# The planner's time allowance for the loads of x that the layer-norm statistics read

## The chip, the cores and the metric

The kernel runs on one core of one Trainium2 chip. The metric is device time in microseconds (us) of one execution, as the median of several runs. A profile is one further execution with its own time.

The engines are named as the profile names them: PE (TensorE, with PEld for its weight loads and PEclk for the clock it was granted), DVE (VectorE), ACT (ScalarE), POOL (GpSimd) and SP (SyncE, which here only issues transfers; "SPq" is its queue).

## The reference

Four layers of graph attention run one after another on 128 graphs of 64 nodes with 512 features, all in float32. Each layer adds to `x` what an attention makes of `h = relu(layernorm(x))`. The graph's adjacency masks the scores. Cut to what matters:

```
h = max(layernorm(x), 0);  x = x + gnn0(h)   # q,k,v (8 heads of 64), masked softmax, values
h = max(layernorm(x), 0);  x = x + gnn1(h)   # the same, and an output projection Wo + bo
h = max(layernorm(x), 0);  x = x + gnn2(h)   # q k^T times adj^T, each row over its norm, times v
h = max(layernorm(x), 0);  x = x + gnn3(h)   # softmax attention, projection o, then o + layernorm(o)
return x
```

`layernorm(x)` is `(x - mean) / sqrt(var + 1e-5)` over the 512 features of a node. The first step of every layer is therefore a read of `x` for mean and variance.

## The kernel before

**Tiling.** The 8192 rows (128 graphs times 64 nodes) are cut into 16 blocks of 512 rows, and a block into four tiles of 128 rows. The four layers make 64 blocks, numbered `n` from 0 to 63; `n // 16` is the layer. `x` between the layers stands in HBM: the input, then a buffer `x1_k` for each block, then the output. Block `n + 1` is loaded and normalized while block `n` is projected.

**One block's way to TensorE.** `load_x` issues four transfers on SP, one for each 128x512 tile `xin` (a ring of four buffers, so a tile of the next block can be loaded only when the tile before it in the same buffer has been used). `layer_norm` takes `bn_stats` and `bn_aggr` of each tile on DVE, then `ve` and `rs = ve ** -0.5` on POOL for the four tiles together, then `nb = -mean * rs` on DVE. ACT then overwrites each tile by `relu(rs * xin + nb)`. `turn` transposes it: DVE splits it into 16-bit halves `z`, SP issues a transposing transfer `hp<-z`, and ACT puts the halves together in `hT`. `sums_x` makes four sums and differences of quarters of `hT` on POOL, the tile `S`.

**Projections.** Each 512x512 weight product is done with seven block products instead of eight, and some of those again with seven quarter products. So PE reads `hT`, `S` and prepared sums of weights, and DVE, ACT and POOL put the partial results together from PSUM (tiles `u`, `s`, `z`, `q`, then `qT`, `kT`, `v`). There are eight PSUM buffers `mm`. Scores, softmax and values follow a block later, interleaved with the next block's projections.

**What sets the order.** Nothing is issued as the code meets it. `Plan.record` writes down every operation with what it depends on, a duration (`duration`, numbers set by hand) and a `late`: how long after the end of the instruction another engine can use the result. `Plan.order` then goes through all steps as a list scheduler: it keeps a time at which each of the five engines is free, picks the step that can start first, and among those that can start, the one of lowest `rank` (its place in the program, moved up for steps that read PSUM or are marked hot). `Plan.issue` issues the steps in that order, so each engine's instruction list is fixed at build time. On the chip every engine runs its own list in that order, and semaphores make it wait for the data. The planner's times are used for nothing else.

For a transfer on SP, `late` comes from line 213, which lets transfers follow each other at 280 bytes a ns (170 for transposes) and start 1400 ns after issue at the earliest, and from line 214, which adds an allowance: `MARGIN` (2000 ns, line 283) for a transposing transfer and 600 ns for every other one. A tile of 128x512 float32 is 262144 bytes.

```
            elif e == "sync":
                moved = max(moved, at + 1400) + late / (170 if calls[0][2].get("transpose") else 280)
                late = moved + (MARGIN if calls[0][2].get("transpose") else 600) - at - busy
```

In addition a transfer depends on the sixteenth-last product that the program recorded before it (`AHEAD`), so that loads aren't issued much too early.

All instructions are issued by `Plan.issue`, so the profile gives line 234 for nearly all of them; they are told apart by their tiles.

Of the kernel before, what the change touches and what calls it, by code (L numbers as in the profile page):

```python
# [59 lines left out]
class Plan:  # L60
# [96 lines left out]
    def order(self):  # L157
        n = len(self.steps)
        wait = [0] * n
        users = [[] for _ in range(n)]  # L160
        for i, s in enumerate(self.steps):
            lags = {**self.lags.get(i, {}), **{d: 0.0 for d in s[2]}}
            wait[i] = len(lags)
            for d, lag in lags.items():
                users[d].append((i, lag))


        rank = [
            i - (n if i in self.front else 0)
            - RUSH * (i in self.hot or any(  # L170
                v.tensor.name.startswith("mm_") for c in s[1] for v in c[1][1:] if isinstance(v, bass.AP)
            ))
            for i, s in enumerate(self.steps)
        ]
        ready = [0.0] * n
        free = {e: 0.0 for e in ("tensor", "vector", "scalar", "gpsimd", "sync")}
        added = 0.0
        moved = 0.0
        port = 0.0
        soon = {e: [] for e in free}  # L180
        here = {e: [] for e in free}
        for i in range(n):
            if not wait[i]:
                heapq.heappush(soon[self.steps[i][0]], (0.0, rank[i], i))
        out = []
        while len(out) < n:
            best = None
            for e in free:
                while soon[e] and soon[e][0][0] <= free[e]:
                    heapq.heappush(here[e], heapq.heappop(soon[e])[1:])  # L190
                if here[e]:
                    at = free[e]
                elif soon[e]:
                    at = soon[e][0][0]
                else:
                    continue
                if best is None or at < best[0]:
                    best = (at, e)
            at, e = best
            if not here[e]:  # L200
                while soon[e] and soon[e][0][0] <= at:
                    heapq.heappush(here[e], heapq.heappop(soon[e])[1:])
            i = heapq.heappop(here[e])[1]
            eng, calls, _, busy, late = self.steps[i]
            moves = calls[0][0] == "dma_start"
            if e == "gpsimd":
                busy += max(0.0, port - at)
            if moves and e == "gpsimd":
                moved = max(moved, at) + 8000
                added = max(added + 6000, at + 8500)  # L210
                late = added - at - busy
            elif e == "sync":
                moved = max(moved, at + 1400) + late / (170 if calls[0][2].get("transpose") else 280)
                late = moved + (MARGIN if calls[0][2].get("transpose") else 600) - at - busy
            elif e == "vector" and late == PORT:
                busy += max(0.0, free["gpsimd"] - at)
                port = at + busy
            free[e] = at + busy
            out.append((at, i))
            for u, lag in users[i]:  # L220
                same = self.steps[u][0] == e
                ready[u] = max(ready[u], at + busy - lag + (0.0 if same and not moves else late))
                wait[u] -= 1
                if not wait[u]:
                    heapq.heappush(soon[self.steps[u][0]], (ready[u], rank[u], u))
        self.start = {i: at for at, i in out}
        self.span = max(free.values())
        return [i for _, i in sorted(out)]
# [54 lines left out]
MARGIN = 2000  # L283
# [1090 lines left out]
```

## Time and profile before

| | |
|---|---|
| median of 3 runs | 2813.59 us (2810.73 to 2822.84) |
| the profiled execution's own time | 2814.77 us |
| its span, first to last instruction | 2813.0 us |
| granted PE clock over the span | 0.999 |
| loads of `xin` | 256, of 256 KB each, on SP |
| DMA, mean over the span | 122 GB/s |

The page's second part cuts the span into 40 equal slices of some 70 us. The layers end at about 690, 1500 and 1960 us. The lines are the busy tenths of each engine, the granted clock in tenths, and what the DMA engines moved:

```profile
PE   9999999999999999999999999999999999999998
DVE  8787576777668778777686665666678778777777
POOL 5666776779767768778689655455777877787875
PEclk9999999999999999999999999999999999999999
GB/s 161 134 155 150 118 178 117 131 147 166 76 111 87 116 93 124 91 97 115 98 133 149 169 168 138 158 143 172 114 80 87 118 93 91 121 104 80 131 78 95
```

A row of the waits reads "engine and tile that waited <- engine and tile (or transfer) that ended the wait: total us, how many times, longest us". A row of the timeline reads "start us, us, engine, line, operation, tile written<-tiles read, shape, count", and in brackets the idle time of the engine before it with what ended it.

### The profile page before, as it was taken

What the parts mean: (1) busy time and instruction counts of PE and PEld (TensorE: products, weight loads), DVE (VectorE), ACT (ScalarE), POOL (GpSimd) and SP (SyncE); (2) the same over time, 40 slices, a digit from 0 to 9 for tenths busy, and PEclk for the clock granted to TensorE, in tenths of its full rate; (3) what the DMA queues carried; (4) which work ended last, traced back from release to release, by engine and by line L of the source; (5) the groups of instructions that cost most, each with busy time, mean ns of one, the idle gap of its engine ahead of it and who ended that gap; (6) DMA issues with size and microseconds to landing.
All of it is one profiled execution on the core that took longest, in us unless ns stands there. A gap on an engine that the chain in (4) does not pass through costs nothing.

```text
span 2813.0 us, 67184 instructions
## 1 busy us (share of the span) xinstructions
PE 2795.0 (99%) x27264; PEld 2484.1 (88%) x27264; DVE 2059.2 (73%) x3900; ACT 1500.7 (53%) x2207; POOL 2014.5 (72%) x2061
## 2 busy tenths in 40 slices
PE   9999999999999999999999999999999999999998
PEld 8888888888889999999998888888888888888887
DVE  8787576777668778777686665666678778777777
ACT  5667566666464554554654444443545545555552
POOL 5666776779767768778689655455777877787875
PEclk9999999999999999999999999999999999999999
DMA  6566485567464656446567775666544644654644
GB/s 161 134 155 150 118 178 117 131 147 166 76 111 87 116 93 124 91 97 115 98 133 149 169 168 138 158 143 172 114 80 87 118 93 91 121 104 80 131 78 95
DMA packets 634599, 343.65 MB, mean 122 GB/s; under 512 B 484273, under 2 KB 565681, under 8 KB 634289
## 3 DMA queue, kind: packets, MB, share of 16 engines
q1 hardware_dynamic: 601024, 273.30, 43.1%
q0 software_dynamic: 33264, 66.06, 14.2%
q8 instruction: 213, 3.49, 0.5%
q14 instruction: 98, 0.79, 0.1%
HBM read 120.10 MB, written 102.76 MB: 79 GB/s over the span
## 4 chain that ended last, share of the span: by engine, by line
PE 95%; DVE 2%; POOL 1%; DMA 1%; issue 1%; SPq 0%; ACT 0%; POOLq 0%; DVEq 0%; ACTq 0%
PE mm L234 95%; SPq L234 0%; POOL S L234 0%; DMA w<-in_L_gnn_Wv_dram 0%; DMA w<-in_L_gnn_Wq_dram 0%; DMA xin<-x 0%; DVE xo L234 0%; DVE sr L234 0%; DVE z L234 0%; POOL rn L234 0%; DVE st L234 0%; DVE qT L234 0%; DVE q L234 0%; DVE w L234 0%; POOL w L234 0%
## 5 line engine op out<-in xcount | busy, mean ns | idle before, releaser
L234 PE MATMUL mm<-S,w 128*128 128x256 f32 (+1 forms) x3680 | 841.6, 377 | 2.0 <-DVE u L234 1.6
L234 PEld LDWEIGHTS mm<-S,w 128*128 128x128 f32 x3680 | 679.8, 190 | 88.6 <-issue 2.3
L234 PE MATMUL mm<-hT,w 128*128 128x256 f32 (+1 forms) x3256 | 601.5, 328 | 3.1 <-DVE q L234 2.8
L234 PEld LDWEIGHTS mm<-hT,w 128*128 128x128 f32 x3256 | 521.8, 191 | 58.6 <-DVE q L234 4.0
L234 DVE TENSOR_TENSOR u<-mm,s 128x512 f32<-128x512 f32 x414 | 284.4, 687 | 292.9 <-PE mm L234 245.3
L234 PE MATMUL mm<-w,S 128*128 128x256 f32 (+1 forms) x2096 | 488.4, 379 | 0.8 <-issue 0.8
L234 PEld LDWEIGHTS mm<-w,S 128*128 128x128 f32 x2096 | 384.2, 190 | 49.9 <-issue 1.2
L234 ACT COPY hT<-hp 128x1024 uint16<-128x1024 uint16 x252 | 330.2, 1358 | 45.3 <-DMA hp<-z 45.1
L234 PE MATMUL mm<-w,hT 128*128 128x256 f32 (+1 forms) x1804 | 346.7, 331 | 0.9 <-DVE q L234 0.8
L234 PEld LDWEIGHTS mm<-w,hT 128*128 128x128 f32 x1804 | 292.8, 191 | 33.7 <-DVE q L234 3.6
L234 DVE COPY z<-xin 128x1024 uint16<-128x1024 uint16 x252 | 255.0, 1023 | 35.4 <-ACT xin L234 29.4
L234 ACT COPY s<-mm 128x512 f32<-128x512 f32 x211 | 123.1, 585 | 288.7 <-PE mm L234 152.9
L234 ACT COPY s<-hp 128x1024 uint16<-128x1024 uint16 x188 | 244.4, 1349 | 3.9 <-DMA hp<-z 3.9
L234 ACT ACTIVATE xin<-xin,nb,rs 128x512 f32<-128x512 f32 x256 | 196.2, 813 | 86.6 <-DVE nb L234 86.6
L234 PE MATMUL mm<-w,SO 128*128 128x256 f32 x992 | 227.1, 379 | 0.0
L234 POOL TENSOR_TENSOR kT<-u,z 128x512 f32<-128x512 f32 x63 | 87.9, 1395 | 182.5 <-DVE u L234 112.7
L234 ACT COPY z<-s 128x1024 uint16<-128x1024 uint16 x188 | 189.6, 1047 | 41.7 <-POOL s L234 41.6
L234 PEld LDWEIGHTS mm<-w,SO 128*128 128x128 f32 x992 | 185.0, 190 | 23.3
L234 POOL TENSOR_TENSOR s<-s,sr 128x1024 f32<-128x1024 f32 x96 | 185.7, 1941 | 25.2 <-DVE nb L234 16.0
L234 POOL TENSOR_TENSOR S<-hT 128x512 f32<-128x512 f32 x126 | 170.3, 1351 | 42.9 <-ACT hT L234 42.9
L234 POOL TENSOR_TENSOR s<-s,mx 128x1024 f32<-128x1024 f32 x96 | 189.5, 2031 | 14.7 <-DVE mx L234 14.7
L234 DVE TENSOR_TENSOR q<-mm,q 128x128 f32<-128x128 f32 x402 | 113.9, 283 | 112.1 <-ACT q L234 96.9
(142 smaller groups left out, 4505.0 us busy)
## 6 DMA issues: line engine op xcount, KB each, us to landing
xin<-x SPq DMA_DIRECT2D x128, 256.0 KB, 3.5
xin<-in_x_dram SPq DMA_DIRECT2D x64, 256.0 KB, 3.4
x<-row POOLq DMA_DIRECT2D x16, 1024.0 KB, 13.4
xin<-out_dram SPq DMA_DIRECT2D x64, 256.0 KB, 4.2
out_dram<-row POOLq DMA_DIRECT2D x16, 1024.0 KB, 14.5
x<-xo POOLq DMA_DIRECT2D x15, 1024.0 KB, 9.3
out_dram<-xo POOLq DMA_DIRECT2D x15, 1024.0 KB, 10.2
xo<-in_x_dram SPq DMA_DIRECT2D x32, 256.0 KB, 4.2
```

What stands on the lines that cost most here:

```text
L234: getattr(getattr(self.nc, eng), op)(*a, **k)
```

## The change

The allowance of 2000 ns, until now for transposing transfers alone, is also used for the loads whose target is a tile `xin`, if the planner places them after its first 20 us. Other loads (weights, rows, `xo`) and the stores keep 600 ns. The condition stands in `Plan.order`:

```
-                late = moved + (MARGIN if calls[0][2].get("transpose") else 600) - at - busy
+
+                margin = calls[0][2].get("transpose") or calls[0][1][0].tensor.name.startswith("xin") and at > 2e4
+                late = moved + (MARGIN if margin else 600) - at - busy
```

The set of instructions, their dependences and their buffers are the same in both kernels. What can differ is the place of each instruction in its engine's list.

## The prediction

> **What bounds the kernel now.** I read the page first, then the waits of TensorE, then the waits of VectorE and the tile `xin`, and last the order of time around the one place where all of them meet. On the page:
>
> ```profile
> span 2813.0 us, 67184 instructions
> PE 2795.0 (99%) x27264; PEld 2484.1 (88%) x27264; DVE 2059.2 (73%) x3900; ACT 1500.7 (53%) x2207; POOL 2014.5 (72%) x2061
> ```
>
> TensorE is busy for 2795.0 of 2813.0 us, and VectorE, the engine that takes the statistics, for 73%. So a wait of VectorE costs time only where it holds up a PSUM eviction long enough to stop TensorE. What TensorE waited for in the whole run:
>
> ```profile
> PE mm L234 <- DVE q L234: 3.6, 3, 2.8
> PE mm L234 <- issue: 2.2, 2, 1.5
> PE mm L234 <- DVE u L234: 1.6, 2, 1.4
> PE mm L234 <- POOL ident masks.py:199: 1.4, 1, 1.4
> PE mm L234 <- DVE v L234: 0.7, 1, 0.7
> PE mm L234 <- ACT z L234: 0.4, 1, 0.4
> PE mm L234 <- ACT oT L234: 0.2, 1, 0.2
> PE mm L234 <- ACT hT L234: 0.2, 1, 0.2
> ```
>
> The columns are total us, times, longest. They sum to 10.3 us: this is all that any better order could take from TensorE by removing such waits, 0.37% of the span. Only the rows that name VectorE's evictions `q` and `u` (5.2 us) can come from a late load of `xin`. VectorE itself waited for those loads in 24 places:
>
> ```profile
> DVE st L234 <- DMA xin<-x: 22.2, 17, 5.4
> DVE st L234 <- DMA xin<-in_x_dram: 5.4, 4, 3.6
> DVE st L234 <- DMA xin<-out_dram: 2.9, 3, 1.2
> DMA to landing us min/median/max: 2.7/3.5/9.9
> ```
>
> Together 30.5 us, before 24 of 256 statistics; the last line is the loads' time from issue to landing. Lines 213 and 214 let the order expect a load 1400 + 262144/280 + 600 ns = 2.94 us after its issue, when nothing is queued ahead of it; half the loads land later than 3.5. The place where one of these waits reaches TensorE, in order of time (start, us, engine, what; in brackets the idle time before it and what ended it), and then the stretches around it, whose last three columns are granted clock, DMA share and GB/s:
>
> ```profile
> 1678.89 0.58 SPq L234 DMA_DIRECT2D xin<-x  x1
> ...
> 1684.26 0.69 DVE L234 BATCH_NORM_STATS2 st<-xin 128x6 f32<-128x512 f32 x1 [3.94 <-DMA xin<-x]
> 1684.87 0.27 DVE L234 TENSOR_TENSOR q<-mm,q 128x128 f32<-128x128 f32 x1
> ...
> 1685.19 0.57 PE L234 MATMUL mm<-hT,w 128*128 128x128 f32 x2 [2.83 <-DVE q L234]
> ```
>
> ```profile
> 1670.00:1690.00 20.00, 17.17 (x82) 14.89 (x81) 12.70 (x25) 8.29 (x12) 12.81 (x14) 0.91 0.93 211
> 1690.00:1735.00 45.00, 44.73 (x409) 39.00 (x408) 27.89 (x68) 16.75 (x26) 25.89 (x30) 1.00 0.53 134
> ```
>
> The load takes 5.34 us (issue at 1678.89 to the statistics at 1684.26), VectorE stands for 3.94 us with the eviction `q` behind it, TensorE stands for 2.83 us, and in these 20 us the granted clock is 0.91 against 1.00 in the next stretch. A pause here costs its length and then some slow matmuls.
>
> **The change, part by part.** It adds no instruction and takes none away. MARGIN is 2000 where 600 stood, so the order now expects a load of `xin` 1.40 us later, 4.34 us after its issue; only loads that the order places in its first 20 us keep the 600. Every step keeps its semaphores, so no wait is added. Everything else follows from the order made with that. I compared the two programs' orders engine by engine: TensorE's last difference is at row 3879 of 6174, VectorE's at 2631 of 3813, ScalarE's at 1377 of 1960, GpSimd's at 1127 of 1780, SyncE's at 683 of 1022. So layer 3, the last third of the time, is as it was and costs nothing either way.
>
> *Removed: VectorE's waits.* A wait of 3.94 us of which 1.40 us is now filled with other work leaves 2.5; TensorE's 2.83 us become 1.4. That is the lower bound of this gain at that place, 1.4 us. The upper bound is the whole of it, 2.83 us and the clock: (1 - 0.91) x 20 us = 1.8 us, together 4.6 us. At 463 us a like case, the statistics 1.39 us late by a load of 3.06 us, stopped TensorE for 0.5 us; 1.39 is under 1.40, so this one goes. Upper bound of all: 5.1 us. The other 22 waits of VectorE hide behind TensorE's queued matmuls, are worth nothing now and nothing when they are gone; the work that hides them is up to eight PSUM banks, and where that cover is gone the price is the one just read, 4.6 us. I take 3.5 us, nearer to the upper end because the neighbouring rows change too: on SyncE the transposes `hp<-z` around this load are put in another order.
>
> The Trainium skill, DMA: Bandwidth & Descriptors, section on the anatomy of one DMA, speaks against the change: a fit of about 2.0 us plus bytes over 436e3, for the software path; for 256 KB an estimate of 2.6 us, by which the old allowance would do and this gain would be zero. The measured medians here, 3.5 us and the 5.34 us of the load that matters, decide against that reading. The skill's TensorE: Matmul & The Clock Gate, part 1, says the clock falls after an idle window of some 3.4 us; the pause here was 2.83 us by the row and the clock fell to 0.91 all the same. By the rule the pause would be worth 2.8 us, by the row 4.6 us.
>
> *Moved: the statistics, and what hangs on them.* Of each block, four BATCH_NORM_STATS2 (0.68 us) and their aggregates move down VectorE's list; behind them stand `ve`, `rs` on GpSimd, `nb`, four activations, four `z` copies, four transposes on SyncE, four `hT` copies on ScalarE, and the sums `S` on GpSimd that TensorE reads. In layers 0 and 2 GpSimd's list changes most: where the four sums `S` (1.27 us each) stood ahead of the two row-max subtractions of the scores (1.90 us each), they now stand behind them in several early blocks. On SyncE the loads of the third and fourth `xin` tile, which stood ahead of the six loads of `xo` in layer 0, now stand behind them; an issue takes about 0.6 us, so 3.7 us. In the old order these sums had time:
>
> ```profile
> 118.70 1.27 POOL L234 TENSOR_TENSOR S<-hT 128x512 f32<-128x512 f32 x1
> 120.06 1.28 POOL L234 TENSOR_TENSOR S<-S,hT 128x512 f32<-128x512 f32 x1
> ...
> 133.42 3.62 PE L234 MATMUL mm<-S,w 128*128 128x256 f32 x16
> ```
>
> The second sum ends at 121.34 and is first read at 133.42, a lead of 12.1 us; sums 3.8 us (two subtractions) and statistics 1.4 to 5 us later still leave a few us. I take zero for layer 0 and keep 1.4 us for each of six blocks, 8.4 us, as the other end. At the entry of layer 2 the lead is thin already:
>
> ```profile
> 1588.57 1.27 POOL L234 TENSOR_TENSOR S<-hT 128x512 f32<-128x512 f32 x1 [4.21 <-ACT hT L234]
> ...
> 1590.59 1.67 PE L234 MATMUL mm<-S,w 128*128 128x256 f32 x7
> ```
>
> The sum ends at 1589.84 and is read 0.75 us later. A chain that is 1.40 us later costs 0.65 us here; five such blocks at the entry give 3.2 us, at worst five times 1.40, 7.0 us; at best nothing, if the list gains elsewhere what it loses there. I take 1.5 us. The end of the run is unchanged.
>
> **Sum.** The profiled execution took 2814.77 us (span 2813.0 and 1.8 around it). Less 3.5, plus 1.5: 2812.8 us. The median of the runs shown, 2813.59, is 1.2 us below that execution, so the forecast is 2811.6, rounded to 2812 us.
>
> **Rivals.** What a measurement of this kernel can tell from no change is about 0.5%, 14.1 us.
>
> *A, forecast: a small gain, 2812 us* (own range 2806 to 2818). For it: the wait at 1684 is in the chain that ended last, and the order now leaves room for it. Chance 0.40.
>
> *B, a wash: 2815 us.* The load at 1678.89 took 5.34 us, over 4.34, so the pause stays in part (1.4 us gained), and the entry of layer 2 pays 3.2 us; 2813.6 - 1.4 + 3.2 = 2815.4. For it: landings up to 9.9 us, and thin leads at 1590. Against: only a few loads exceed 4.34 by much. The change would then do what it says for VectorE and nothing for TensorE. Chance 0.30.
>
> *C, slower: thin leads turn into pauses with a slowed clock, 2832 us.* The place is the first blocks of layer 0, where the sums now stand behind the subtractions, and the entry of layer 2. As long as a sum is under a us late it costs that; a pause of near 3 us costs 4.6 us as at 1684. It decides from the fourth such pause on: 4 x 4.6 = 18.4 us over 2813.6. For it: one late load can delay all that hangs on it, and `xin`'s third and fourth tile are now issued later. Against: the lead of 12.1 us. Chance 0.22.
>
> *D, faster beyond the measurement: 2799 us.* It would need 14.1 us, where all waits of TensorE are 10.3 us and the clock lost at 1684 is 1.8 us; 12.1 us in all, 2801.5 us. So this needs short gaps inside the matmul stream to close too, which nothing in the profile ties to these loads. Chance 0.08.
>
> **How the numbers follow.** A and B lie within 0.5%: same 0.70; slower is C, 0.22; faster is D, 0.08. The range reaches from all of the gain, 2813.6 - 5.1 = 2808.5, less the 2.9 us by which the lowest run lies below the median, 2805.6, up to no gain with both worst costs, 2813.6 + 7.0 + 8.4 = 2829.0. C begins where it exceeds the measurement, at 2827.7, and its middle is 2832; to leave out no more than D and about half of C, under 2 in 10, I give 2805 to 2831.
>
> **What would show it.** Right: VectorE's waits for `xin` fall from 30.5 us to under 15; the row `PE mm <- DVE q` falls from 3.6 us to about 1; the clock in the stretch around 1680 us is nearer to 1.00; TensorE busy stays within a few us of 2795. Wrong in the step on sums: rows `PE mm <- POOL S` or `ACT hT` that are not there now, in layer 0 before 450 us or at 1500 to 1620 us, and stretches there with a clock under 1.00. Wrong in the first step: the pause at 1684 stands with the same load ahead of it. What makes the whole wrong is several new pauses of about 3 us.

## The result, and the profile after

| | before | after |
|---|---|---|
| median of 22 runs each, same chip | 2812.33 us (2810.69 to 2822.84) | 2817.61 us (2815.90 to 2819.64) |
| after / before, 95% interval | | 1.0016 [1.0009, 1.0023] |
| own time of the profiled execution | 2814.77 us | 2818.18 us |
| its span | 2813.0 us | 2816.4 us |
| granted PE clock over the span | 0.999 | 0.999 |

The changed kernel is slower by 0.16%. The interval excludes both a gain and a loss of 0.5%: small, but not of the sign that was forecast. In the first part of the page, the span and the busy times of the engines:

```profile
span 2816.4 us, 67187 instructions
PE 2794.6 (99%) x27264; PEld 2484.0 (88%) x27264; DVE 2033.6 (72%) x3900; ACT 1498.8 (53%) x2207; POOL 2012.9 (71%) x2061
```

TensorE is busy for 0.4 us less than before (2795.0) and the span is 3.4 us longer: the work did not grow, the gaps did. VectorE's waits for the loads of `xin`, after (total us, times, longest):

```profile
DVE st L236 <- DMA xin<-in_x_dram: 8.6, 4, 3.4
DVE st L236 <- DMA xin<-x: 4.4, 8, 1.2
DVE st L236 <- DMA xin<-out_dram: 2.6, 3, 1.1
```

They went from 30.5 us in 24 places to 15.6 us in 15, so the allowance did what it says. What TensorE waited for, after:

```profile
PE mm L236 <- DVE q L236: 7.3, 6, 4.4
PE mm L236 <- issue: 1.9, 2, 0.9
PE mm L236 <- POOL ident masks.py:199: 1.4, 1, 1.4
PE mm L236 <- ACT xin L236: 0.7, 2, 0.5
PE mm L236 <- DVE v L236: 0.7, 1, 0.7
PE mm L236 <- POOL SO L236: 0.7, 1, 0.7
PE mm L236 <- POOL hT L236: 0.6, 1, 0.6
```

The row for the evictions `q` was to fall from 3.6 us to about 1. It rose to 7.3, and one wait in it is of 4.4 us. It does not lie at 1684 us. The windows of after around the old place and around the new one (window; wall and PE busy; PEld; DVE; ACT; POOL; then granted clock, DMA share and GB/s):

```profile
860.00:880.00 20.00, 15.61 (x72) 13.55 (x71) 15.60 (x23) 4.89 (x8) 15.09 (x16) 0.91 0.63 105
...
1670.00:1690.00 20.00, 20.00 (x197) 17.75 (x196) 12.48 (x32) 7.86 (x15) 11.91 (x14) 1.00 0.53 145
```

The pause at 1684 is gone, and its stretch has the full clock. A larger pause stands in the middle of layer 1, where the same 20 us were full before:

```profile
860.00:880.00 20.00, 20.00 (x112) 18.09 (x111) 14.01 (x29) 10.66 (x19) 16.23 (x18) 1.00 0.78 132
```

**Where the 3.4 us come from.** TensorE has the same 27264 matmuls in every kernel, so the time that it loses can be worked out from the trace: the distance between the starts of two neighbouring groups of matmuls, less the first quartile of that distance over all groups of the same size, summed by stretch. It counts pauses as well as matmuls slowed by the clock. In every kernel of this study the span is 2770.7 us plus the total of this table (all in us):

| stretch | before | after | difference |
|---|---|---|---|
| 0–40 | 3.2 | 3.3 | +0.1 |
| 40–300 (layer 0) | 4.2 | 6.4 | +2.2 |
| 300–600 (layer 0) | 5.2 | 4.9 | −0.3 |
| 600–850 | 5.2 | 4.8 | −0.4 |
| **850–900 (layer 1)** | **0.4** | **6.5** | **+6.1** |
| 900–1500 | 4.8 | 5.0 | +0.2 |
| 1500–1650 (entry of layer 2) | 1.8 | 3.0 | +1.2 |
| **1650–1750 (layer 2)** | **6.2** | **0.6** | **−5.6** |
| 1750–1960 | 2.4 | 1.6 | −0.8 |
| 1960–2780 and end | 8.9 | 9.5 | +0.6 |
| total | 42.3 | 45.7 | +3.4 |

So the gain is there, and larger than the 3.5 us that the sum took; one single place in layer 1 takes all of it back, and layer 0 and the entry of layer 2 cost a little more.

**The place in layer 1.** VectorE and GpSimd in the order of time, before (start us, us, engine, line, operation, tile<-tiles read, shape):

```profile
862.34 1.34 POOL L234 DMA_DIRECT2D x<-xo  x1
...
862.50 0.28 DVE L234 TENSOR_TENSOR w<-w 128x128 f32<-128x128 f32 x1
...
863.99 4.79 POOL L234 TENSOR_TENSOR s<-s,mx 128x1024 f32<-128x1024 f32 x2
```

and after:

```profile
863.76 1.35 POOL L236 DMA_DIRECT2D x<-xo  x1
...
864.26 6.10 DVE L236 TENSOR_TENSOR w<-w 128x128 f32<-128x128 f32 x1
...
864.64 1.78 POOL L236 DMA_DIRECT2D x<-row  x1
...
865.41 4.79 POOL L236 TENSOR_TENSOR s<-s,mx 128x1024 f32<-128x1024 f32 x2
...
871.95 0.27 DVE L236 TENSOR_TENSOR q<-mm,q 128x128 f32<-128x128 f32 x1
...
872.28 1.65 PE L236 MATMUL mm<-w,oT 128*128 128x128 f32 x6 [4.39 <-DVE q L236]
```

The instruction `w<-w` is one of the sums of weights that are made once per layer, 128x128, both operands in SBUF, the on-chip buffer in which `xin` stands too. Before, it started 0.16 us after GpSimd's first transfer issue and took 0.28 us. After, it started 0.50 us after that issue and took 6.10 us: until GpSimd was through with two transfer issues and both row-max subtractions (865.41 + 4.79 = 870.20). The eviction `q` stands behind it and behind two statistics (871.95), and TensorE stands for 4.39 us. No load is late here, and no sum `S` either. The prediction had no term for this.

### The profile page after: what moved, and what is told of

Read it like the earlier page. It is cut to its first block, busy times and chain, and to the rows that moved or that the text cites. A ratio compares the mean times of both kernels' runs of the same rounds, so it can differ in the third digit from the quotient of the medians.

```text
span 2816.4 us, 67187 instructions
## 1 busy us (share of the span) xinstructions
PE 2794.6 (99%) x27264; PEld 2484.0 (88%) x27264; DVE 2033.6 (72%) x3900; ACT 1498.8 (53%) x2207; POOL 2012.9 (71%) x2061
## 5 line engine op out<-in xcount | busy, mean ns | idle before, releaser
L236 DVE COPY z<-xin 128x1024 uint16<-128x1024 uint16 x252 | 238.0, 958 | 41.7 <-ACT xin L236 31.5
L236 POOL TENSOR_TENSOR s<-s,sr 128x1024 f32<-128x1024 f32 x96 | 183.8, 1923 | 24.0 <-DVE nb L236 15.6
L236 PE MATMUL mm<-w,oT 128*128 128x256 f32 (+1 forms) x994 | 188.1, 335 | 4.6 <-DVE q L236 4.4
```

The lines of the kernel that those rows point to most:

```text
L236: getattr(getattr(self.nc, eng), op)(*a, **k)
```

## The experiments

All were timed in 11 runs beside 33 of the kernel before on the same chip (median 2813.80 us for the first four, 2813.65 for the last four). The theory: an engine's list decides what an eviction waits behind, and the cost is VectorE instructions that GpSimd holds up, standing ahead of an eviction `q`. The rivals: later statistics make the sums `S` late (the prediction's own third case), and the size of the allowance itself is the dose.

### e3_layer2: the allowance in layer 2 alone

```
-                margin = calls[0][2].get("transpose") or calls[0][1][0].tensor.name.startswith("xin") and at > 2e4
+                margin = calls[0][2].get("transpose") or calls[0][1][0].tensor.name.startswith("xin") and at > 1.48e6
```

> The larger allowance is used for the loads of layer 2 alone. The order of layers 0 and 1 is then that of the kernel before, the order of layer 2 that of the kernel after. Theory (three separate places: a gain at the entry of layer 2, one long wait of VectorE for GpSimd in layer 1, thin leads in layer 0): the pause of TensorE near 1684 us is gone and the one near 866 us does not come, so the time is 4.7 us below the kernel before, near 2807.6 us, and the row PE mm <- DVE q falls from 3.6 to under 1.5 us. If the pause near 1684 us belonged to that one execution only, the gain is 1 to 2 us. Rival (later statistics cost everywhere, and the pause near 866 us is one instance): 2812 to 2816 us.

Measured: 2808.41 us (2806.92 to 2811.28), ratio 0.9983 [0.9974, 0.9992], faster by 0.17%. The span is 2807.8 us. Of the time lost, 1650 to 1750 us fell from 6.2 to 0.7, 850 to 900 stayed at 0.4. The stretch of the old pause:

```profile
1670.00:1690.00 20.00, 20.00 (x123) 17.70 (x125) 14.98 (x31) 8.67 (x15) 11.88 (x16) 1.00 0.65 162
```

So the gain that was forecast for this place is real: 5.5 us less lost in this stretch. Without the other layers' new order it is not given back.

### e1_layer0: the allowance in layer 0 alone

```
-                margin = calls[0][2].get("transpose") or calls[0][1][0].tensor.name.startswith("xin") and at > 2e4
+                margin = calls[0][2].get("transpose") or calls[0][1][0].tensor.name.startswith("xin") and 2e4 < at < 6.9e5
```

> The larger allowance is used for the loads that the order places before 690 us, which are layer 0's and layer 1's first. The order of layer 0 is that of the kernel after, that of layer 2 that of the kernel before, and layer 1 gets an order of its own, in which the sum w<-w stands elsewhere. Theory: layer 0 alone costs 2.3 us (0.6 us in each of some five blocks, less one gain near 460 us), so 2814.6 us, if layer 1's new order has no long wait for GpSimd. Rival (layer 0 holds most of the loss): 2817 us or more.

Measured: 2815.63 us (2811.88 to 2818.78), ratio 1.0005 [0.9996, 1.0014]. That is 1 us above what was expected, and the interval holds 1, so the sum over layer 0 is not shown by the time. In layer 0 its order is that of after. The trace shows 6.7 us lost from 40 to 300 us (before 4.2, after 6.4), and the pause at 1684 is back (1650 to 1750: 5.7). TensorE's waits in 40 to 300 us name the evictions `q` (2.0 us in four), once `hT` of GpSimd (0.6) and never `S`. After has the same rows there (1.7 and 0.6 us). In time, one of these places in after:

```profile
95.68 3.76 POOL L236 TENSOR_TENSOR s<-s,sr 128x1024 f32<-128x1024 f32 x2
95.74 1.85 DVE L236 SCALAR_TENSOR_TENSOR nb<-mv,rs 128x4 f32<-128x4 f32 x1 [1.31 <-POOL rs L236]
...
98.48 1.51 DVE L236 COPY z<-xin 128x1024 uint16<-128x1024 uint16 x1 [0.88 <-ACT xin L236]
99.91 0.28 DVE L236 TENSOR_TENSOR q<-mm,q 128x128 f32<-128x128 f32 x1
100.24 2.02 PE L236 MATMUL mm<-hT,w 128*128 128x128 f32 x11 [0.53 <-DVE q L236]
```

`nb` is 512 numbers and takes 1.85 us: until the first of the two GpSimd instructions ends (95.68 + half of 3.76 = 97.56). The copy `z`, 0.68 us when alone (the next at 100.71), takes 1.51 us, until shortly after the second ends (99.44). Then comes the eviction, and TensorE has stood for 0.53 us. In the kernel before, `nb` was as slow (median of the 21 before 700 us: 1055 ns, after 1083 ns). But there this block's `nb` ran at 78.84 us and its first `z` at 85.51, long before its `q` (98.32). The long duration is old; what is new is that the statistics, and `nb` and `z` with them, have moved down to just ahead of the eviction.

Layer 1 has an order of its own in this run, and it shows a second case. The same two transfer issues and two GpSimd instructions of 128x1024 hold up another sum with both operands in SBUF for as long as `w<-w`:

```profile
868.87 6.08 DVE L236 TENSOR_TENSOR hT<-hT 128x128 f32<-128x128 f32 x1
```

Yet TensorE has no wait from 850 to 900 us, its clock is 1.00, and 0.5 us are lost. It still had matmuls to do until the next eviction `q` (875.08). So here a hold-up of 6 us cost nothing; in after and e5 it has an eviction behind it that TensorE needs at once.

### e4_move: after, with one instruction moved

```
-        for i in self.order():
+        todo = self.order()
+        todo.remove(3566)
+        todo.insert(todo.index(3585) + 1, 3566)
+        for i in todo:
```

Step 3566 is the `w<-w` at 864 us, step 3585 a `q<-q` later in VectorE's list.

> The kernel after, with one VectorE instruction moved: the 128x128 sum w<-w that took 6.10 us at 864 us stands behind the q<-q that follows GpSimd's row-max subtractions, at about 874 us. Theory: the wait is VectorE's for GpSimd (two transfers' issue and two subtractions, 863.8 to 870.2 us) and takes 4.4 us of TensorE and 1.8 us of clock with it; the instruction then takes under 1 us, the clock of that stretch is 1.00, and the time is 6 us below the kernel after, near 2811.5 us. Rival (the late statistics are the cause, the sum only stands among them): the pause stays and the time is within 1.5 us of 2817.6 us.

Measured: 2811.75 us (2811.08 to 2814.86), ratio 0.9993 [0.9984, 1.0002]: from after's 1.0016 that is 0.23%, 6.5 us, by moving one VectorE instruction of 3900. It now takes 0.28 us:

```profile
868.57 1.48 DVE L240 TENSOR_TENSOR q<-q 128x128 f32<-128x128 f32 x1
...
869.98 0.28 DVE L240 TENSOR_TENSOR w<-w 128x128 f32<-128x128 f32 x1
```

and the stretch is full again, at the full clock:

```profile
860.00:880.00 20.00, 20.00 (x109) 18.00 (x108) 14.70 (x29) 10.36 (x19) 17.17 (x18) 1.00 0.78 133
```

The row above it tells the same: `q<-q`, the same shape with both operands in SBUF, took 1.48 us while GpSimd's subtractions ran. It ended at 870.05, 0.16 us after them (865.10 + 4.79 = 869.89), as `w<-w` did in after (870.36 and 870.20); behind it `w<-w` started when they were over.

### e5_late: before, with the same instruction moved the other way

```
-        for i in self.order():
+        todo = self.order()
+        todo.remove(3566)
+        todo.insert(todo.index(3615) + 1, 3566)
+        for i in todo:
```

The allowance is 600 ns as before; step 3615 is one statistics instruction.

> The kernel before, with the same VectorE sum w<-w moved down by one statistics instruction, from 862.5 to about 863.3 us, when GpSimd has begun to issue its transfers. Nothing else differs, the allowance neither. Theory: it is caught until the second row-max subtraction ends near 868.8 us, takes 4 to 6 us, and TensorE pauses; the time is 3 to 6 us above the kernel before, 2815.5 to 2818.5 us. Rival: no change, 2811 to 2813.5 us.

Measured: 2819.15 us (2816.70 to 2821.39), ratio 1.0014 [1.0004, 1.0023]. That is 5.4 us over the medians of before (expected: 3 to 6), 3.9 by the ratio. Moved by one statistics instruction, the sum of 0.28 us takes 5.84, and the whole of after's pause appears in the kernel before, with no load's allowance touched:

```profile
864.10 5.84 DVE L238 TENSOR_TENSOR w<-w 128x128 f32<-128x128 f32 x1
...
871.65 1.14 PE L238 MATMUL mm<-w,oT 128*128 128x128 f32 x6 [4.52 <-DVE q L238]
```

```profile
860.00:880.00 20.00, 15.48 (x71) 13.24 (x71) 14.83 (x23) 4.19 (x7) 15.81 (x18) 0.91 0.65 105
```

Lost between 850 and 900 us: 6.8 (before 0.4, after 6.5, e4 0.3). With e4 this settles which instruction's place brings layer 1's pause.

### e6_moves: e4 and six places of layer 0

To e4's move come nine. Six put a VectorE instruction (`nb` once, `z<-xin` five times) behind the eviction that it held up, at the blocks near 98, 139, 179, 217, 262 and 597 us of after. The other three take along the transfer that reads the moved `z`; SyncE's own order stays. Only VectorE's list differs.

```
+        for a, b in [(3566, 3585), (455, 418), (456, 455), (613, 589), (797, 760), (798, 797), (968, 923), (1139, 1102), (1140, 1139), (2542, 2499)]:
+            todo.remove(a)
+            todo.insert(todo.index(b) + 1, a)
```

> The kernel after, with the sum w<-w moved as in the run before, and in six blocks of layer 0 (near 98, 139, 179, 217, 262 and 597 us) the VectorE instruction that stood caught behind GpSimd (nb or the copy z<-xin) moved behind the PSUM eviction that it held up. Only VectorE's list differs. Theory (layer 0's loss is evictions standing behind a VectorE instruction that waits for GpSimd's row-max or row-sum product): these places lose 0.4 to 0.7 us each, near 597 us 1.4, and give back about 3 us against 2811.75: near 2809 us. Rival, the prediction's step (the sums S come too late for TensorE): moving the copies down makes the sums later still, so nothing is gained or the time rises: 2812 us or more, with rows PE mm <- POOL S.

Measured: 2809.18 us (2808.13 to 2811.26), ratio 0.9985 [0.9976, 0.9994]. Beside e4 (0.9993) the intervals overlap, so the further gain is not shown by the time alone; the medians differ by 2.6 us and the spans by 3.2 (2809.6 and 2806.4). TensorE's waits:

```profile
PE mm L240 <- DVE u L240: 2.0, 2, 1.8
PE mm L240 <- DVE q L240: 0.2, 1, 0.2
```

The row for `q` is down from 3.4 us in e4 to 0.2. But one move failed: at 139 us `nb` (1.86 us), put behind `q`, and after it `z` (1.51 us) hold up the eviction `u` that follows at 143.40. TensorE, let go earlier by `q`, stands for 1.8 us there, more than the 0.4 us that it lost at this block in after. Another place for `nb` was not tried.

### e7_stat: before, with one statistics instruction moved

```
+        for a, b in [(7059, 6958)]:
+            todo.remove(a)
+            todo.insert(todo.index(b) + 1, a)
```

Step 7059 is the `st<-xin` of 1684 us, step 6958 the eviction `q`. The allowance stays at 600 ns. This asks whether the pause at 1684 comes from the late load, or from the eviction's place behind it.

> The kernel before, with one VectorE instruction moved: the statistics that waited 3.94 us for its load at 1684 us now stand one place further down, behind the eviction q that they held up. Allowance and all else are as before. Theory (the place in the list costs, not the load): TensorE gets its PSUM bank some 4 us earlier, the pause of 2.83 us becomes under 1 us, the clock stays at 1.00, and the time is 3 to 4.7 us below the kernel before, 2809 to 2810.5 us. Rival (the load's late landing holds the next evictions as well, so the pause only moves by one instruction): 2812 us or more.

Measured: 2810.78 us (2809.14 to 2813.46), ratio 0.9989 [0.9980, 0.9997], just above the expected 2809 to 2810.5. The order of time there:

```profile
1680.66 0.29 DVE L238 TENSOR_TENSOR q<-mm,q 128x128 f32<-128x128 f32 x1 [0.86 <-ACT q L238]
...
1683.07 0.70 DVE L238 BATCH_NORM_STATS2 st<-xin 128x6 f32<-128x512 f32 x1 [2.12 <-DMA xin<-x]
```

VectorE still waits 2.12 us for the load, and it costs TensorE nothing at once: the stretch 1670 to 1690 has the clock 1.00 and PE busy throughout. Some of it may move on, since 1650 to 1750 us still loses 2.4 us (before 6.2, after 0.6).

### m700: an allowance of 700 ns instead of 2000

```
-                late = moved + (MARGIN if margin else 600) - at - busy
+                late = moved + (MARGIN if calls[0][2].get("transpose") else 700 if margin else 600) - at - busy
```

> The allowance for xin is 700 ns, 100 more than before instead of 1400. The order differs from the one before in few places (16 of the list places in layers 0 and 1, 30 in layer 2), and one of these is the swap of the run with one statistics moved. Theory: 3 to 4.7 us below the kernel before, as there: 2809 to 2810.5 us. Rival (the size of the allowance counts): a fourteenth of any effect, 2812.5 to 2814 us.

Measured: 2808.38 us (2805.93 to 2810.25), ratio 0.9981 [0.9972, 0.9990], a little better than expected. With 100 ns more the kernel is 0.19% faster, with 1400 ns more 0.16% slower. 100 ns can't absorb a load that is 3.94 us late; among other moves it does in the list what e7 does by hand, it puts that statistics instruction behind `q` (1650 to 1750 us: 1.8). In layer 1 it leaves `w<-w` where it was unharmed (850 to 900 us: 0.4). What its other moves give is not shown; beside e7 the intervals overlap. So the time does not follow the allowance as a dose. Each value draws another order, and at the two places that were tested the time follows what that order puts ahead of an eviction. Values between and beyond these were not tried.

### e8_both: layer 2's allowance, and six moves in layer 0

e3, with five VectorE instructions of layer 0 put behind the eviction that stood after them in e3's own order. The sixth move takes along a ScalarE instruction that reads one of them; ScalarE's own order stays.

```
-                margin = calls[0][2].get("transpose") or calls[0][1][0].tensor.name.startswith("xin") and at > 2e4
+                margin = calls[0][2].get("transpose") or calls[0][1][0].tensor.name.startswith("xin") and at > 1.48e6
...
+        for a, b in [(293, 254), (1653, 1576), (1666, 1653), (1479, 1405), (2016, 1985), (2035, 1992)]:
+            todo.remove(a)
+            todo.insert(todo.index(b) + 1, a)
```

> The larger allowance for layer 2's loads alone (2808.4 us), and in layer 0 five VectorE instructions that stand caught behind GpSimd (near 54, 342, 382, 474 and 478 us) moved behind the eviction that they hold up. Theory: these places lose 2.0, 0.5, 1.0 and 1.4 us; half to all of it comes back: 2804 to 2806.5 us. Rival (these short waits are hidden or move on to the next eviction): 2808 us.

Measured: 2807.21 us (2806.14 to 2808.78), ratio 0.9978 [0.9970, 0.9987], the lowest of all, but above the expected 2804 to 2806.5. The page, and the wait row for `q`:

```profile
span 2805.1 us, 67191 instructions
PE 2791.5 (100%) x27264; PEld 2482.5 (89%) x27264; DVE 2050.1 (73%) x3900; ACT 1501.4 (54%) x2207; POOL 2015.1 (72%) x2061
```

```profile
PE mm L240 <- DVE q L240: 0.4, 1, 0.4
```

It is faster than both kernels, but against e3 (0.9983) the intervals overlap: the moves' own part, 2.7 us by the spans, is not shown by the time, and the rival's 2808 us is not excluded. The time lost, in the stretches that matter (us):

| | 40–300 | 300–600 | 850–900 | 1500–1650 | 1650–1750 | total | median us |
|---|---|---|---|---|---|---|---|
| before | 4.2 | 5.2 | 0.4 | 1.8 | 6.2 | 42.3 | 2812.3 to 2813.8 |
| after | 6.4 | 4.9 | 6.5 | 3.0 | 0.6 | 45.7 | 2817.6 |
| e1_layer0 | 6.7 | 5.2 | 0.5 | 1.8 | 5.7 | 44.0 | 2815.6 |
| e3_layer2 | 4.9 | 6.6 | 0.4 | 2.0 | 0.7 | 37.1 | 2808.4 |
| e4_move | 6.8 | 4.4 | 0.3 | 3.0 | 0.7 | 38.9 | 2811.8 |
| e5_late | 4.6 | 5.8 | 6.8 | 1.8 | 5.0 | 48.9 | 2819.2 |
| e6_moves | 5.0 | 3.3 | 0.3 | 3.2 | 0.8 | 35.7 | 2809.2 |
| e7_stat | 2.8 | 5.8 | 0.3 | 1.8 | 2.4 | 37.3 | 2810.8 |
| m700 | 3.9 | 4.7 | 0.4 | 1.8 | 1.8 | 35.9 | 2808.4 |
| e8_both | 2.7 | 4.8 | 0.4 | 2.0 | 0.7 | 34.4 | 2807.2 |

The table also tells how far one profile can be trusted. Before, e3, e5 and e7 have the same order in layer 0, and lose 4.2, 4.9, 4.6 and 2.8 us from 40 to 300 us (mean 4.1), and 5.2, 6.6, 5.8 and 5.8 from 300 to 600 (mean 5.9). After, e1 and e4 share the other order: 6.4, 6.7 and 6.8 (mean 6.6), and 4.9, 5.2 and 4.4 (mean 4.8). So the new order costs layer 0 about 2.5 us in its first blocks and gives 1.0 us back in the next, some 1.5 us in all; a difference under 2 us between two single profiles says little.

## Why the prediction went the wrong way

**What bounds the kernel** held. TensorE is busy for 2794.6 us where 2795 was expected, and the two large changes, 6.1 and 5.6 us, are waits behind VectorE's evictions. The measured time lies inside the range that was given, but by luck: a gain larger than forecast and a loss that had no term nearly cancel.

**"Removed: VectorE's waits"** had the right place and the right chain (late load, eviction `q`, TensorE, clock), and too small a value. Taken: 3.5 us, with 5.1 us as the upper bound. Measured: the stretch 1650 to 1750 us loses 6.2, 5.7 and 5.0 us with the old order there (before, e1, e5) and 0.6 to 0.8 with the new one (after, e3, e4, e6, e8), so 5.0 us by the means, the upper end. The waits for `xin` fell to 15.6 us (expected under 15), and the clock near 1680 is 1.00. What the working had wrong is how the gain comes about. It subtracted 1.40 us of allowance from a wait of 3.94 and asked what stays. But a list order has no such subtraction: by e7 and m700 the statistics go behind `q` or they don't, and once they do, most of the wait is off TensorE's path (in after they stand at 1695.52, behind `q` at 1688.67). The lower bound of 1.4 us, and with it the wash at 2815 us, rested on that subtraction.

**"Moved: the statistics, and what hangs on them"** is the step that failed. It followed the moved instructions to what needs their results: `ve`, `rs`, `nb`, the transposes, `S`. It priced layer 0 at zero because `S` has a lead of 12.1 us, and layer 2's entry at 1.5 us.

- The entry of layer 2 had about the right size, +1.2 us, but not by late sums `S`: TensorE's new wait from 1500 to 1650 us is `POOL SO` (0.7 us), sums of `oT`, beside `ACT hT` (0.2 us), which before had too. Its cause isn't settled: e3, whose allowance begins at 1480 us of the planner's time, loses 0.2 us more than before there, so it comes only with an order that differs ahead of it.
- In layer 0 the lead of `S` held; no row `PE mm <- POOL S` appeared, and of the chain only `POOL hT`, once, 0.6 us. The profiles put a cost of about 1.5 us there all the same (40 to 600 us: means of 11.5 and 10.0), though it is not clear of their scatter: e3, with the old order, has 11.5 too. In the places that were looked at, it comes by a way that the step did not look at: `nb` and `z` now stand just ahead of an eviction on VectorE, and GpSimd holds them up. The bound of 8.4 us covered the amount; its mechanism was another.
- In layer 1 the sum had no term at all. The 6.1 us there are more than the whole gain. The instruction isn't among the statistics or anything that hangs on them: it is a sum of weights that was shifted by 0.34 us against GpSimd's list. By e4 and e5, one instruction's place accounts for it in both directions.

In the two profiles the terms are −5.6 us (1650–1750), +6.1 (850–900), +1.9 (40–600), +1.2 (entry of layer 2) and −0.2 (all the rest): +3.4 us, as the spans have it; the medians of 22 runs are 5.3 us apart.

**The rivals.** Case C named the sign but neither the size (2832 us) nor the way: it wanted four pauses near 3 us from late sums, where there was one pause of 4.39 us with the clock at 0.91 (the price of 4.6 us for a pause of 2.83 was of the right kind: this one cost 6.1), and no late sum. Case B had the smallness right and the reasons wrong. Case D's doubt, that no more than the waits of 10.3 us and some clock can be won, stands: the best version is 6.4 us below before by the medians.

What could have been seen beforehand: before's trace had VectorE instructions with both operands in SBUF that took several times their usual time while GpSimd ran (`nb`, 512 numbers: 127 to 1859 ns, median 1055). A step "where does a VectorE instruction with two SBUF operands stand, what does GpSimd run then, and which eviction is behind it" looks at places of this kind. That it would have named this one is not shown: `w<-w` follows the same eviction `u` in both kernels (861.90 and 863.65), and 0.34 us decide.

The planner isn't blind to the wait. `duration` marks 16-bit copies, and instructions with two SBUF operands of more than 64 numbers a row, with `PORT` (`z` and `w<-w` are among them), and `Plan.order` lengthens these until the GpSimd instruction that is running ends; GpSimd's next one then waits for VectorE. So it reckons with one GpSimd instruction, where `w<-w` was held over four. `nb`, with four numbers a row, gets a fixed 120 ns and no such wait.

The Trainium skill, SBUF — State Buffer, section on who interferes with whom, says that a VectorE instruction with two SBUF inputs contends with a GpSimd instruction that reads SBUF, that copies can contend in their fast modes too, and that the port pair which the two engines share is an exclusive lock: in those modes the one that is first holds it for the whole instruction. The traces agree in kind: `nb` 1.85 us, `z` 1.51 us, `w<-w` 6.10 us, while in e4 the statistics, with one SBUF input, took their usual 0.66 us at 864.00 next to the first of the same GpSimd instructions, and `u<-mm,s`, with one SBUF input as well, its usual 0.69 us at 867.65 next to the subtractions. In the length they agree for `nb` at 95.74, which ended with one GpSimd instruction, and differ for `w<-w`: that hold-up went on over four in a row.

## What to carry to other kernels

In a list made by a scheduler, price an instruction that shifts against another engine's list by what stands behind it on its own engine and by what the other engines run at that moment, not only by who needs its result. The size of a scheduling allowance is no dose: 100 ns and 1400 ns had opposite signs here, so a change of this sort is a new draw of the order and must be measured by stretch, where gains and losses of 6 us each hide behind a net of 3. If one instruction decides, move that instruction, and look again at the eviction that then stands behind it.

## What the runs showed of the hardware

- A 128x128 sum on VectorE with both operands in SBUF took 0.28 us, or 6.10 (after), 5.84 (e5) and 6.08 us (e1) when it started 0.50 to 0.76 us after a GpSimd transfer issue with another issue and two GpSimd instructions of 128x1024 to follow. Each time it ended 0.15 or 0.16 us after the last of these. That GpSimd holds it is read from these times; no run took GpSimd's instructions away.
- In these three places VectorE got no turn between four GpSimd instructions in a row. That isn't so everywhere: `nb` at 95.74 in after got its turn between two (it ended at 97.59, the first of them at 97.56). What makes the difference stays open.
- The time since GpSimd's issue doesn't decide alone. Started 0.16 us after the issue, `w<-w` went through (before). So did a sum of the same shape with two SBUF operands 0.91 us after another issue, behind which GpSimd had nothing to do until 1073.61:

```profile
1070.86 1.28 POOL L234 DMA_DIRECT2D x<-row  x1
...
1071.77 0.28 DVE L234 TENSOR_TENSOR S<-hT,S 128x128 f32<-128x128 f32 x1
```

- TensorE's granted clock was 0.91 over 20 us with a pause of 2.83 us (before), 4.39 us (after) and 4.52 us (e5). This is a mean. Before's windows show the full clock up to the pause and in it, about half of it for some 3.5 us behind it, and then the full clock again:

```profile
1680.00:1685.00 5.00, 2.37 (x14) 1.81 (x12) 1.06 (x3) 2.09 (x4) 0.63 (x1) 1.00 1.01 172
1685.50:1689.00 3.50, 3.50 (x13) 3.00 (x12) 1.58 (x4) 0.98 (x1) 2.41 (x3) 0.52 1.03 278
1689.00:1692.00 3.00, 3.00 (x16) 2.64 (x15) 2.07 (x6) 0.66 (x2) 0.00 (x0) 1.00 0.00 1
```

- That is 1.7 us (0.48 x 3.5). The time lost in all by the pauses of after and e5 was 6.1 and 6.4 us (over 0.4), so 1.7 and 1.9 us beyond the pause itself. A pause of 1.8 us (e6, to 144.13 us) left the clock at 1.00 from 144 to 150 us.
